# Layer 2 of a four-layer graph kernel: statistics over four batches, small copies on ScalarE, own entries of the mask behind the last sums

## The chip, the cores and the metric

One core of a Trainium2 chip runs the whole program. The metric is the device time of one execution, in microseconds (us). Before the change the median of three runs is 1942.64 us (1941.84 to 1944.92).

Five engines work side by side, each through its own list of instructions in order: TensorE (PE; its weight loads are PEld) multiplies and transposes into the accumulators (PSUM), VectorE (DVE) and ScalarE (ACT) do the elementwise work, GpSimd (POOL) reduces over partitions, SyncE (SP) issues the transfers. They wait for each other by semaphores.

## The reference, cut to what matters

`x` holds 16 batches of 1024 nodes with 64 features, `adj` the 1024 x 1024 adjacency of all batches. Four graph layers follow each other, each in the form `x = layernorm(x + layer(x))`. The change lies in the third, layer 2:

```python
h = inp @ W
s1, s2 = h @ a1, h @ a2                       # one score per node
e = leaky_relu(s1[:, None] + s2[None, :], 0.2)
attention = softmax(where(adj > 0, e, NEG))
x = layernorm(inp + elu(attention @ h))       # mean and variance over the 64 features
```

Layer 3 then uses the same adjacency with its diagonal set (every node is its own neighbour):

```python
mask = graph + eye(N) > 0
scores = where(mask, h @ h.T, NEG)            # four heads, and an outer layer
```

## The kernel before

A batch's 1024 nodes lie as 8 chunks (C) of 128 partitions. The weights aren't formed as a row-wise softmax: since exp(leaky(s1 + s2)) is the larger of two products of exponentials, VectorE builds, for one chunk k of neighbours, `e = max(G, q) * aT` in one instruction over 128 x 1024 (`unit`, L1011). G (exponentials of s1) serves two batches, a *pair*, as do p and q (exponentials of s2 beneath the largest s2); aT is the transposed adjacency in bfloat16. TensorE adds up the products of e with `vals` = x * p over the eight chunks (`product`, L1019); one column of vals holds p itself, so the sums of the softmax come out with the products.

`gat_layer` (L911) writes layer 2's order by hand: for each batch t and chunk k there is a slot. In a slot a unit is issued on VectorE, then the product of the unit two slots back on TensorE, then the slot's tasks in the order in which they were put there. `go` (L1219) emits it in a stretch where the scheduler may not move the four compute engines. So every engine's queue follows the order of the slots, and within a slot the order of the calls of `at`: first the loop over the batches' ends (L1180 to L1189), then the loop over the pairs' preparation (L1191 to L1215). The tasks:

- Ends of batch b (list at L1157, places from L1172): `evict` copies the products yT to SBUF (ACT); `project` multiplies with W and brings the nodes back to partitions (PE, tile po); `divide` (L1083) takes the sums out of po, clamps them on DVE into `sums` (kept for a later check) and takes the reciprocal rt (DVE); `quotients` scales po by rt in eight instructions into v and takes exp(v) into m (ACT); `residual` makes elu and adds x (two DVE instructions); `norm` takes `bn_stats` of each chunk (DVE) and, after each odd batch, `moments` (L754) for the pair's 16 columns; `root` takes the inverse root by Ln and Exp (ACT); `shift` refines it (four DVE instructions with the shift); `store` writes the normalized rows into x by eight ACT instructions (`scaled`, L776; recorded at L780). The last four batches store by two DVE instructions (L1152).
- Preparation of a pair (L1193): `prep_x` transposes x (PE) and copies xT (ACT, L934); `prep_s` makes the scores s1, s2 (PE, tile ps); `prep_top` (L945) copies them to SBUF (DVE), takes the maximum of s2 (DVE) and sends it to POOL for the maximum over partitions, gtop; `prep_p` (L955) makes -gtop and 0.8 gtop (DVE, `down` and `up`) and the exponentials p and q (ACT); `prep_G` (L989) makes s1 for all partitions in two halves (PE, tile pg) and their exponentials G (ACT, L987); `prep_v` (L993) scales x by p into vals in eight ACT instructions and copies p.

Layer 1's last stores (`last`, L2004) and layer 3's first preparation (`ahead`, L2065) are put into layer 2's first and last slots by `extra` (L2093). Layer 3's preparation there is `prep_x` (L1347: transposes, and copies xT at L1354), `prep_h` (L1362: hT), `prep_sq` (L1378: squares) and `shift_of` (L1325). Before layer 3 the diagonal of aT is set in eight DVE instructions (L2105 to L2107), which stand outside the hand-written stretch: the scheduler placed them between layer 2's last units. Layer 3's heads (L1384) then run bursts of scores (PE), exponentials (ACT, L1397), masks (DVE, L1401) and products (PE, L1408).

Of the kernel before, what the change touches and what calls it, by code (L numbers as in the profile page):

```python
# [8 lines left out]
F32 = mybir.dt.float32  # L9
# [4 lines left out]
ALU = mybir.AluOpType  # L14
AX = mybir.AxisListType

P = 128
FLT_MAX = 3.4028234e38
LN_EPS = 1e-5
ALPHA = 0.2  # L20
# [562 lines left out]
def fast_path(  # L583
# [24 lines left out]
    nc = tc.nc  # L608
    B, N, D = x.shape
    C = N // P  # L610
# [3 lines left out]
    GB = 4  # L614
# [6 lines left out]
    small = ctx.enter_context(tc.tile_pool(name="small", bufs=4))  # L621
    ep = ctx.enter_context(tc.tile_pool(name="ep", bufs=2))
# [6 lines left out]
    for g in range(NG):  # L629
        t = xpool.tile([P, C, GB, D], F32, tag=f"x{g}", name=f"x{g}")  # L630
# [16 lines left out]
    ident16 = const.tile([P, P], BF16, tag="ident16", name="ident16")  # L647
# [106 lines left out]
    def moments(st):  # L754


        n = st.shape[1]
        t = {k: small.tile([P, n], F32, tag=f"bn_{k}", name=f"bn_{k}") for k in ("mean", "d", "var", "rstd", "shift")}
        v = nc.vector
        v.tensor_tensor(t["d"], st[:, :, 1], st[:, :, 4], ALU.subtract)  # L760
        v.tensor_tensor(t["var"], st[:, :, 2], st[:, :, 5], ALU.add)
        v.tensor_tensor(t["mean"], st[:, :, 1], st[:, :, 4], ALU.add)

        v.scalar_tensor_tensor(t["d"], t["d"], 0.25, t["d"], ALU.mult, ALU.mult)
        v.tensor_scalar(t["var"], t["var"], 1.0 / D, LN_EPS, ALU.mult, ALU.add)
        v.tensor_tensor(t["var"], t["var"], t["d"], ALU.add)
        root, step = inverse_root(t["rstd"], t["var"])

        def finish():
            step()  # L770
            v.scalar_tensor_tensor(t["shift"], t["mean"], -0.5, t["rstd"], ALU.mult, ALU.mult)  # L771
            return t["rstd"], t["shift"]

        return root, finish
# [136 lines left out]
    def gat_layer(w, name, zero_mean, own, room=None):  # L911
# [33 lines left out]
        def prep_top(b):  # L945
            pt = pq[b]
            s = s12[:, b // 2]
            nc.vector.tensor_copy(s, pt[:, : 4 * C].rearrange("p (c f) -> p c f", f=4))
            top = small.tile([P, 1], F32, tag="top", name="top")
            nc.vector.tensor_reduce(top, s[:, :, 2:4], AX.XY, ALU.max)  # L950
            gtop = small.tile([P, 1], F32, tag="gtop", name="gtop")
            nc.gpsimd.partition_all_reduce(gtop, top, P, bass_isa.ReduceOp.max)
            pq[b] = gtop

        def prep_p(b):  # L955
            gtop = pq[b]
            down = small.tile([P, 1], F32, tag="down", name="down")
            nc.vector.tensor_scalar(down, gtop, -1.0, None, ALU.mult)
            up = small.tile([P, 1], F32, tag="up", name="up")
            nc.vector.tensor_scalar(up, gtop, 1.0 - ALPHA, None, ALU.mult)  # L960
            s2 = s12[:, b // 2, :, 2:4]
            p = small.tile([P, C, 2], F32, tag="p", name="p")
            nc.scalar.activation(p, s2, AF.Exp, bias=down)
            q = small.tile([P, C, 2], F32, tag="q", name="q")
            nc.scalar.activation(q, s2, AF.Exp, bias=up, scale=ALPHA - 1.0)
            pq[b] = (p, q, up)
# [38 lines left out]
        def attention(b):  # L1005
            held = {}
            pair = stats.setdefault(b // 2, {})
            joint = not zero_mean and b < B - 2
            begins, closes = b % 2 == 0 or not joint, b % 2 == 1 or not joint

# [72 lines left out]
            def divide():  # L1083
                pos, tot = held["p"]
                held["v"] = ep.tile([P, C, D], F32, tag="v", name="v")
                if not zero_mean:
                    if begins:
                        n = 2 if joint else 1
                        total = sums[:, b : b + n, :]
                        nc.vector.tensor_scalar(  # L1090
                            total.rearrange("p u (h j) -> p u h j", h=2),
                            pair["tot"].rearrange("p j (u h) -> p u h j", h=2), 1e-30, None, ALU.max,
                        )
                        pair["r"] = small.tile([P, n, C], F32, tag="rt0", name="rt")
                        nc.vector.reciprocal(pair["r"], total)
                    held["r"] = pair["r"][:, b % 2 if joint else 0, :]
                    quotients()
                    return
                total = sums[:, b, :]
                nc.vector.tensor_scalar(total.rearrange("p (h t c) -> p t c h", h=2, t=2), tot, 1e-30, None, ALU.max)  # L1100
                rt = small.tile([P, C], F32, tag="rt", name="rt")
                nc.vector.reciprocal(rt, total)
                held["r"] = rt

            def quotients():
                pos, rt = held["p"][0], held["r"]
                for h, po in enumerate(pos):
                    if zero_mean:

                        for j in range(CH):  # L1110
                            c = h * CH + j
                            nc.scalar.activation(
                                held["v"][:, c, :], po[:, j // 2, j % 2, :], AF.Copy, scale=rt[:, c : c + 1]
                            )
                        continue
                    nc.vector.tensor_tensor(
                        held["v"][:, h * CH : (h + 1) * CH, :].rearrange("p (t c) d -> p t c d", t=2), po,
                        rt[:, h * CH : (h + 1) * CH].rearrange("p (t c) -> p t c", t=2).unsqueeze(3).to_broadcast(
                            [P, 2, 2, D]
                        ), ALU.mult,  # L1120
                    )
                held["m"] = ep.tile([P, C, D], F32, tag="m", name="m", bufs=4)
                nc.scalar.activation(held["m"], held["v"], AF.Exp)

            def residual():
# [3 lines left out]
                nc.vector.scalar_tensor_tensor(m, m, 1.0, v, ALU.min, ALU.add)  # L1129

            def norm():
                if b % 2 == 0:
                    pair["st"] = small.tile([P, 2 * C, 6], F32, tag="bn", name="bn")
                st = pair["st"]
                for c in range(C):
                    nc.vector.bn_stats(st[:, b % 2 * C + c, :], held["m"][:, c, :])
                if b % 2:
                    pair["end"] = moments(st)

            def root():  # L1140
                if b % 2:
                    stats[b // 2]["end"][0]()

            def shift():
                if b % 2:
                    stats[b // 2]["n"] = stats[b // 2]["end"][1]()

            def store():
                rows = slice(b % 2 * C, (b % 2 + 1) * C)
                rstd, shift = (t[:, rows] for t in stats[b // 2]["n"])  # L1150
                if zero_mean and b >= B - 4:
                    nc.vector.tensor_tensor(held["m"], held["m"], bc_last(rstd, D), ALU.mult)  # L1152
                    nc.vector.tensor_tensor(xb(b), held["m"], bc_last(shift, D), ALU.add)
                    return
                scaled(xb(b), held["m"], (rstd, shift), range(C))
# [24 lines left out]
        for b in range(B):  # L1180
            places = ends[b % 2]
            if not zero_mean and b % 2 == 0 and b < B - 2:
                places = [(1, 3), (2, 5), (2, 7), (3, 0), (3, 1), (3, 1), (3, 1), (4, 0)]
            if zero_mean and b == B - 4:
                places = [*places[:-1], (4, 3)]
            if zero_mean and b == B - 1:
                places = [(1, 0), (1, 1), (1, 1), (1, 1), *places[4:]]
            for task, (t, k) in zip(work[b][2], places):
                at(b + t, k, task)  # L1189
# [680 lines left out]
    with tc.tile_pool(name="ps_g", bufs=1, space=bass.MemoryType.PSUM, reuse_waits="tile") as ps_g, tc.tile_pool(  # L1870
# [45 lines left out]
        extra = {}  # L1916
# [173 lines left out]
    with tc.tile_pool(name="ps_g", bufs=1, space=bass.MemoryType.PSUM, reuse_waits="tile") as ps_g, tc.tile_pool(  # L2090
        name="ps_p", bufs=1, space=bass.MemoryType.PSUM, reuse_waits="tile"
    ) as ps_p:
        places = [(15, j) for j in (0, 1, 2, 3, 4, 5, 6, 7)]  # L2093
        extra = {p: [task] for p, task in zip(places, ahead)}
        for p, task in zip(((0, 0), (0, 1), (0, 3), (0, 7), (1, 3), (1, 7)), last):
            extra.setdefault(p, []).append(task)

        ending = l2_go(extra)
    gat.close()
    for j, task in enumerate(ending):  # L2100
        at(0, j, task)

    for c in range(C):  # L2105
        own = aT[:, c, c * P : (c + 1) * P]
        nc.vector.tensor_tensor(own, own, ident16, ALU.max)  # L2107

    early.close()
    l3 = ctx.enter_context(tc.tile_pool(name="l3", bufs=2, reuse_waits="tile"))  # L2110
# [11 lines left out]
    for b in range(B):  # L2122
        units = work[b][0][0] + work[b][1][0]
        outer = outs[b - 1][1][0] if b else []
        for j in range(BURSTS):
            n = (2, 2, 3, 5)[j - 4] if b >= E - 1 and j >= 4 else 5 if j < 4 else 3
            burst, units = units[:n], units[n:]
            m = 5 - n
# [101 lines left out]
```

## Time and profile before

One execution was profiled. Its rows are read against its own time.

| what | us |
|---|---|
| median of three runs | 1942.64 |
| time of the profiled execution | 1941.5 |
| its span, first to last instruction | 1939.5 |
| PE, DVE, ACT, POOL busy in the span | 1869.1, 1762.0, 1322.1, 78.4 |
| DVE units of layers 0 and 2 (L1013, 256) | 315.6, 1275 ns each |
| ACT exponentials of layer 3's heads (L1397, 512) | 538.9, 1123 ns each |
| DVE masks of layer 3's heads (L1401, 512) | 596.1, 1215 ns each |
| ACT rows of `scaled` (L780, 224) | 77.5, 430 ns each |

The first unit of layer 2 starts at 422.7 us, its last at 629.5 us. A timeline row gives start, length, engine, source line, operation, output tile, input tiles, shapes and count; in brackets it may give the idle time before it and what ended that. Tile names leave the layer out (G_l, y_l). A row with a count holds several instructions in a chain: neighbouring instructions of one engine overlap by some tens of ns, so that the distance from start to start, not the length, is what one of them costs its engine.

### The profile page before, as it was taken

What the parts mean: (1) busy time and instruction counts of PE and PEld (TensorE: products, weight loads), DVE (VectorE), ACT (ScalarE), POOL (GpSimd) and SP (SyncE); (2) the same over time, 40 slices, a digit from 0 to 9 for tenths busy, and PEclk for the clock granted to TensorE, in tenths of its full rate; (3) what the DMA queues carried; (4) which work ended last, traced back from release to release, by engine and by line L of the source; (5) the groups of instructions that cost most, each with busy time, mean ns of one, the idle gap of its engine ahead of it and who ended that gap; (6) DMA issues with size and microseconds to landing.
All of it is one profiled execution on the core that took longest, in us unless ns stands there. A gap on an engine that the chain in (4) does not pass through costs nothing. (4 is left out here: it accounts for less than half of the span.)

```text
span 1939.5 us, 25733 instructions
## 1 busy us (share of the span) xinstructions
PE 1869.1 (96%) x9505; PEld 761.3 (39%) x9505; DVE 1762.0 (91%) x2997; ACT 1322.1 (68%) x2316; POOL 78.4 (4%) x77
## 2 busy tenths in 40 slices
PE   8999989989888999999999999999999999999996
PEld 4444347763333333333333333333333333333332
DVE  6899988879999888799998998989989899899997
ACT  4566568767767676777767767677666776776763
POOL 0000000000000000000000000000000000000001
PEclk8999989999999999999999999999999999999998
DMA  7000000000000110000000100000000100001000
GB/s 181 1 1 1 1 1 1 1 1 1 1 1 12 41 59 12 12 16 24 12 18 12 29 17 12 17 18 23 18 12 18 28 12 17 12 18 29 12 23 13
DMA packets 45746, 35.87 MB, mean 18 GB/s; under 512 B 37295, under 2 KB 37616, under 8 KB 45614
## 3 DMA queue, kind: packets, MB, share of 16 engines
q1 hardware_dynamic: 43534, 33.64, 6.6%
q8 instruction: 76, 1.25, 0.3%
q10 hardware_dynamic: 2080, 0.52, 0.1%
q14 instruction: 56, 0.46, 0.1%
HBM read 29.45 MB, written 4.70 MB: 18 GB/s over the span
## 5 line engine op out<-in xcount | busy, mean ns | idle before, releaser
L1397 ACT ACTIVATE e<-s,shift 128x1024 f32<-128x1024 f32 x512 | 538.9, 1123 | 239.2 <-PE s L1393 237.3
L1401 DVE TENSOR_TENSOR e<-e,aT 128x1024 f32<-128x1024 f32 x512 | 596.1, 1215 | 5.9 <-ACT e L1397 5.9
L1393 PE MATMUL s<-hT 64*128 64x512 f32 x2048 | 489.3, 602 | 2.7 <-ACT zT L1440 1.4
L1408 PE MATMUL y<-e,vals 128*64 128x512 f32 x2048 | 483.4, 599 | 2.0 <-DVE e L1401 1.1
L1013 DVE SCALAR_TENSOR_TENSOR e<-G_l,q,aT 128x1024 f32<-128x1024 f32 x256 | 315.6, 1275 | 2.2 <-ACT G_l L987 2.0
L1393 PEld LDWEIGHTS s<-hT 64*128 64x128 f32 x2048 | 183.6, 185 | 288.2 <-issue 143.5
L1025 PE MATMUL y_l<-e,vals_l 128*64 128x512 f32 x1024 | 254.9, 615 | 29.2 <-DVE e L1013 22.4
L1408 PEld LDWEIGHTS y<-e,vals 128*64 128x64 f32 x2048 | 135.2, 136 | 269.1 <-issue 197.8
L1577 DVE TENSOR_TENSOR e<-e,aT 128x1024 f32<-128x1024 f32 x128 | 156.3, 1225 | 11.2 <-ACT e L1564 1.6
L1569 DVE SCALAR_TENSOR_TENSOR junk<-e,aN 128x1024 bf16<-128x1024 f32 x120 | 146.1, 1217 | 0.0
L1564 ACT ACTIVATE e<-s,shift 128x1024 f32<-128x1024 f32 x128 | 138.6, 1114 | 2.4 <-PE s L1559 2.4
L1559 PE MATMUL s<-h2T 64*128 64x512 f32 x512 | 125.8, 591 | 0.0
L1585 PE MATMUL y<-e,h2v 128*64 128x512 f32 x512 | 125.6, 592 | 0.0
L1025 PEld LDWEIGHTS y_l<-e,vals_l 128*64 128x64 f32 x1024 | 61.5, 137 | 161.0 <-issue 76.4
L1950 PE MATMUL po<-hi,aR 128*128 128x512 f32 x256 | 102.6, 402 | 10.1 <-ACT hi L1862 6.3
L1336 POOL PARTITION_ALL_REDUCE gtop<-top x48 | 55.0, 1145 | 1255.9 <-DVE top L1334 985.9
L1950 PE MATMUL po<-lo,aR 128*128 128x512 f32 x256 | 101.0, 395 | 0.0
L780 ACT ACTIVATE x<-m,bn_shift,bn_rstd 128x64 f32<-128x64 f32 x224 | 77.5, 430 | 15.6 <-DVE bn_shift L771 15.6
L1559 PEld LDWEIGHTS s<-h2T 64*128 64x128 f32 x512 | 50.1, 186 | 60.1 <-issue 37.4
L1440 ACT COPY zT<-poT 64x512 f32<-64x512 f32 x124 | 72.0, 581 | 1.1
L1415 ACT COPY yT<-y 128x512 f32<-128x512 f32 x64 | 38.5, 601 | 43.7 <-PE y L1408 42.5
L1585 PEld LDWEIGHTS y<-e,h2v 128*64 128x64 f32 x512 | 36.6, 137 | 73.6 <-issue 58.5
(279 smaller groups left out, 1888.7 us busy)
## 6 DMA issues: line engine op xcount, KB each, us to landing
r<-inverse SPq DMA_DIRECT2D x62, 256.0 KB
adj<-in_adj_dram SPq DMA_DIRECT2D x16, 512.0 KB
out_dram<-res SPq DMA_DIRECT2D x15, 256.0 KB
x<-in_x_dram SPq DMA_DIRECT2D x14, 256.0 KB
rows<-yT SPq DMA_DIRECT2D x62, 4.0 KB
x<-in_x_dram ACTq DMA_DIRECT2D x2, 256.0 KB
sums<-rows SPq DMA_DIRECT2D x31, 8.0 KB
inverse<-rt SPq DMA_DIRECT2D x31, 8.0 KB
```

Of the source, the lines that this page charges most:

```text
L1013: nc.vector.scalar_tensor_tensor(e, G[b - b % 2][:, b % 2, :], pq[b - b % 2][1][:, k, b % 2 : b % 2 + 1], aT[:, k, :], ALU.max, ALU.mult,)
L1025: nc.tensor.matmul(held["y"][h * D : (h + 1) * D, :], vals[b][:, k, :], e[:, h * HALF : (h + 1) * HALF], start=(k == 0), stop=(k == C - 1),)
L1393: nc.tensor.matmul(s[:, i, :], hT[rows, k * P : (k + 1) * P], hT[rows, cols], start=True, stop=True)
L1397: nc.scalar.activation(e, s, AF.Exp, bias=shifts[b, n])
L1401: nc.vector.tensor_tensor(e, e, bc_mid(aT[:, k, h * HALF : (h + 1) * HALF], 2), ALU.mult)
L1408: nc.tensor.matmul(held[h][i * D : (i + 1) * D, :], vals[b][:, k, :], e[:, i, :], start=(k == 0), stop=(k == C - 1),)
L1559: nc.tensor.matmul(s[:, i, :], hT[rows, (i + k // CH) % 2, k % CH * P : (k % CH + 1) * P], hT[rows, 0, :], start=True, stop=True,)
L1564: nc.scalar.activation(e, s, AF.Exp, bias=shifts[b])
L1569: nc.vector.scalar_tensor_tensor(junk.rearrange("p c q -> p (c q)").bitcast(BF16), e.rearrange("p i q -> p (i q)"), 1.0, aN[:, k, :], ALU. ...
L1577: nc.vector.tensor_tensor(e, e, aT[:, k, :].rearrange("p (i q) -> p i q", i=2), ALU.mult)
L1585: nc.tensor.matmul(held["o"][h * D : (h + 1) * D, :], vals["out", b][:, k, :], e[:, h, :], start=(k == 0), stop=(k == C - 1),)
L1950: nc.tensor.matmul(po.rearrange("p q k f -> p (q k f)"), aR[:, k, ic * P : (ic + 1) * P], e[:, k].rearrange("p q k f -> p (q k f)"), start ...
```

## The change

In layer 2 (`zero_mean`) alone, but for the last point:

1. `norm`, `root`, `shift` and `store` work on groups of four batches instead of two, for the first twelve batches; the last four stay in pairs. The statistics' tile of a group has 32 columns, and it and the tile m of those batches come from the layer's own pool, m with 6 buffers. The four stores of a group stand at new places: for its first to last batch at (b + 5, slot 6), (b + 5, slot 0), (b + 4, slot 4), (b + 4, slot 0).
2. `prep_top` takes the maximum straight from PSUM on DVE; the copy of the scores to SBUF goes to ACT, behind it.
3. `prep_p` makes down and up on ACT.
4. `divide` takes the reciprocal straight from PSUM on DVE, without the clamp; the copy of the sums, which only the later check reads, goes to ACT, behind it.
5. The own entries of the mask are set in slot (16, 1), inside the hand-written stretch, behind the last batch's `divide`.

```diff
         def prep_top(b):
...
+            if zero_mean:
+                nc.vector.tensor_reduce(top, got[:, :, 2:4], AX.XY, ALU.max)
+                nc.scalar.copy(s, got)
...
         def prep_p(b):
...
+            if zero_mean:
+                nc.scalar.mul(down, gtop, -1.0)
+                nc.scalar.mul(up, gtop, 1.0 - ALPHA)
...
         def attention(b):
...
+            four = zero_mean and b < B - 4
+            size = GB if four else 2
+            mine = b % size
+            group = stats.setdefault((size, b // size), {})
...
             def divide():
...
-                total = sums[:, b, :]
-                nc.vector.tensor_scalar(total.rearrange("p (h t c) -> p t c h", h=2, t=2), tot, 1e-30, None, ALU.max)
                 rt = small.tile([P, C], F32, tag="rt", name="rt")
-                nc.vector.reciprocal(rt, total)
+                for where, put in ((rt, nc.vector.reciprocal), (sums[:, b, :], nc.scalar.copy)):
+                    put(where.rearrange("p (h t c) -> p t c h", h=2, t=2), tot)
...
-                held["m"] = ep.tile([P, C, D], F32, tag="m", name="m", bufs=4)
+                pool, bufs = (gp, 6) if four else (ep, 4)
+                held["m"] = pool.tile([P, C, D], F32, tag="m", name="m", bufs=bufs)
...
             def norm():
-                if b % 2 == 0:
-                    pair["st"] = small.tile([P, 2 * C, 6], F32, tag="bn", name="bn")
-                st = pair["st"]
+                if mine == 0:
+                    group["st"] = (gp if four else small).tile([P, size * C, 6], F32, tag="bn", name="bn")
+                st = group["st"]
                 for c in range(C):
-                    nc.vector.bn_stats(st[:, b % 2 * C + c, :], held["m"][:, c, :])
-                if b % 2:
-                    pair["end"] = moments(st)
+                    nc.vector.bn_stats(st[:, mine * C + c, :], held["m"][:, c, :])
+                if mine == size - 1:
+                    group["end"] = moments(st)
...
+            if zero_mean and b < B - 4:
+                places = [*places[:-1], ((5, 6), (5, 0), (4, 4), (4, 0))[b % GB]]
...
+        def own_nodes():
+            for c in range(C):
+                own = aT[:, c, c * P : (c + 1) * P]
+                nc.vector.tensor_tensor(own, own, ident16, ALU.max)
+
+        extra.setdefault((B, 1), []).append(own_nodes)
         ending = l2_go(extra)
...
-    for c in range(C):
-        own = aT[:, c, c * P : (c + 1) * P]
-        nc.vector.tensor_tensor(own, own, ident16, ALU.max)
```

`root`, `shift` and `store` use `group` and `mine` in the same way as `norm`.

## The prediction

> **What bounds the kernel now.** I read the stretches by time first, then the waits of VectorE inside layer 2, then the timelines of VectorE and ScalarE over one pair of batches. Columns of the first view: stretch, length, busy time and count of PE, PEld, DVE, ACT, POOL, then clock, DMA share, GB/s.
>
> ```profile
> 430.00:632.00 202.00, 179.83 (x861) 66.50 (x860) 197.53 (x410) 144.25 (x468) 10.54 (x9) 0.99 0.01 3
> 700.00:1300.00 600.00, 599.16 (x2928) 219.33 (x2930) 545.25 (x708) 426.08 (x550) 26.70 (x23) 1.00 0.07 17
> ```
>
> The reader is to see that layer 2 (422 to 634 us) belongs to VectorE, 197.5 of 202 us, and layer 3 to TensorE without a gap. Layer 3 starts from layer 2's last product, so what layer 2 gains or loses moves the end one for one. Next, what VectorE waits for from 422 to 632 us:
>
> ```profile
> DVE e L1013 <- ACT G_l L987: 2.0, 1, 2.0
> ```
>
> One wait in the whole stage: a unit (the product e of one chunk) that waits for ScalarE's exponential G. Apart from that VectorE runs back to back, so its costs are read from start to start of neighbouring rows. VectorE over one pair:
>
> ```profile
> 484.10 0.18 DVE L948 COPY l_s<-ps 128x32 f32<-128x32 f32 x1
> 484.32 0.17 DVE L950 TENSOR_REDUCE top<-l_s 128x1 f32<-128x16 f32 x1
> 484.41 1.28 DVE L1013 SCALAR_TENSOR_TENSOR e<-G_l,q,aT 128x1024 f32<-128x1024 f32 x1
> ...
> 490.15 0.15 DVE L958 TENSOR_SCALAR down<-gtop 128x1 f32<-128x1 f32 x1
> 490.21 0.14 DVE L960 TENSOR_SCALAR up<-gtop 128x1 f32<-128x1 f32 x1
> 490.27 3.67 DVE L1013 SCALAR_TENSOR_TENSOR e<-G_l,q,aT 128x1024 f32<-128x1024 f32 x3
> 493.86 0.16 DVE L1100 TENSOR_SCALAR l_sums<-po 128x8 f32<-128x8 f32 x1
> 494.06 0.20 DVE L1102 RECIPROCAL rt<-l_sums 128x8 f32<-128x8 f32 x1
> 494.18 1.23 DVE L1013 SCALAR_TENSOR_TENSOR e<-G_l,q,aT 128x1024 f32<-128x1024 f32 x1
> 495.33 0.17 DVE L712 SCALAR_TENSOR_TENSOR ln_step<-bn_rstd 128x16 f32<-128x16 f32 x1
> ...
> 496.04 3.67 DVE L1013 SCALAR_TENSOR_TENSOR e<-G_l,q,aT 128x1024 f32<-128x1024 f32 x3
> ```
>
> The third unit of the last row (two starts of 1.19 on: 498.43) is the first of the next pair; it reads the new G. ScalarE beside it:
>
> ```profile
> 493.79 1.11 ACT L987 ACTIVATE G_l<-pg,up 128x1024 f32<-128x1024 f32 x1 [0.60 <-PE pg L978]
> 494.80 1.74 ACT L1112 ACTIVATE v<-po,rt 128x64 f32<-128x64 f32 x8
> 496.57 0.63 ACT L1123 ACTIVATE m<-v 128x512 f32<-128x512 f32 x1
> 497.11 1.10 ACT L987 ACTIVATE G_l<-pg,up 128x1024 f32<-128x1024 f32 x1
> 498.11 2.75 ACT L780 ACTIVATE x<-m,bn_shift,bn_rstd 128x64 f32<-128x64 f32 x8
> ```
>
> The second half of G ends at 498.21, 0.22 us before the unit that needs it. That margin decides this change. The chain to it starts at unit U (490.27): its product and the scores pg on TensorE let G's first half start at U+3.52, and G, eight v, m and G end at U+7.94. VectorE needs it at U+8.16. All seven pairs show it but the first, where ScalarE is late by the 2.0 us above.
>
> **What VectorE saves.**
> - Sums: the clamp goes, the reciprocal reads PSUM itself. Not in the trace; nearest rows: from PSUM 0.16 (clamp), reciprocal 0.20. Start to start 0.32 becomes 0.12 to 0.20; I take 0.12, since the drop of the clamp's hand-over (493.86 to 494.06) is sure: 0.20 a batch.
> - down and up: 490.15 to 490.27, 0.12 to 0.13 a pair.
> - Scores: copy and maximum take 0.31 from 484.10; a maximum straight from PSUM lies between 0.09 (its spacing now) and 0.20; I take 0.10, its own row's: 0.20 saved a pair.
> - Statistics: a pair's cost 0.88 (moments) + 0.71 (495.33 to 496.04) = 1.59. With 32 columns layer 1's tail shows both: 421.69 to 422.72 = 1.03, and 425.11 to 425.89 = 0.78; 1.81 in all. Six pairs become three groups: 6 x 1.59 - 3 x 1.81 = 4.1 us.
> - Own entries: of eight (0.13 each where nothing hides them), six stood ahead of the last unit and cost about 0.3 there. Behind the last reciprocal they take 8 x 0.13 = 1.0 us, in VectorE's idle 3.5 us before layer 3's first mask (637.77): free. Without that cover, 1.0.
>
> Summed over the stage, nearly 10 us. But three new things stand in ScalarE's queue.
>
> **Wait 1: the copy of the sums.** In the changed program's order it stands on ScalarE right ahead of G's first half (even batches) or of the next batch's vals (odd), and it waits for VectorE; v behind it carries no wait of its own any more, so the copy's wait is the one for the reciprocal, issued before it. That ends at U+3.59+0.20; every v in the trace starts 0.10 after rt (453.92+0.20 to 454.22). The copy isn't in the trace: between 0.09 (L999's spacing, 128x8) and 0.47 (L934's, 128x512 from PSUM); nearest is L999, 0.10. So G starts at U+3.99 instead of U+3.52: **0.47 us later**, and v, m and second G behind it.
>
> [...]
>
> In odd batches vals (2.0) now stand behind rt, where they ran before it: from the pair's first unit X, rt at X+8.32, copy, vals, v (1.78), m end at X+13.2, and the residual wants them at X+13.68-0.40 = X+13.28. Just free; I take 0, at worst 0.15 in each of 7 pairs.
>
> **Wait 2: the store ahead of G.** The stores of the first batch of a group are placed in the same slot as the second half of G, and stand first in the order: eight of L780, 498.11 to 500.76 = 2.65 us, ahead of what the next unit needs. It happens three times (G of batches 6, 10, 14).
>
> So, with a hand-over of 0.03 (G's end 445.37 to unit 445.40), the next pair's first unit waits:
> - pairs with a group's end: G at U+8.41+2.65 = U+11.06; VectorE there at 8.16-0.20+0.07 = U+8.03. Stall 3.06.
> - pairs without: G at U+8.41; VectorE at 8.16-0.20-0.71 = U+7.25. Stall 1.19: what the missing step saves is waited away.
>
> Balance of a pair (26.51 now, 471.92 to 498.43). Without group's end: -0.40-0.20-0.13-1.59+1.19 = -1.13. With: -0.40-0.20-0.13+0.15+0.07+3.06 = +2.55. Together +1.42, three times: **+4.3 us**. The other three stores follow within the pair; by the same adding up they delay the copies yT to X+15.9 at most, and the product po needs it at X+17.0: free.
>
> **First pair.** ScalarE is the bound from 435.25 to 445.37. p waits 0.20 for down now; down and up there cost 0.2 to 0.5 (128x1 rows of L1341 last 0.29; p to q is 0.21 apart), and the sums 0.10: **+0.3 us**, and VectorE's savings before it are lost.
>
> **Wait 3: the end.** From the last pair's first unit (X = 604.48) ScalarE runs a store, yT, a store, then the copy after rt (X+8.63), vals, v, m to X+13.07, and now one more store, 2.65, to X+15.7, before the copies xT of layer 3's first transposes. TensorE's phT started at X+14.18 (618.66); it now waits to X+16.3, and all products of batch 15 stand behind it in TensorE's queue. TensorE is busy from there to the last product but for 0.59+0.20 us, so 2.1-0.8 = +1.3 remains; clamp and hand-over less, copy more, -0.1: **+1.2 us**. The queues of SP and POOL keep their order, no transfer moves.
>
> **Sum:** 4.3+0.3+1.2 = +5.8 us. The profiled execution took 1941.5 (span 1939.5 and 2.0 around it): 1947.3. The median of the runs is 1.1 above that execution: **1948.4 us**.
>
> **Rivals.**
> - Faster. Place: the first unit of a pair. If G's second half were there by U+7.25 and U+8.03, nothing would be given back: per four batches -2.32-0.51, three times -8.5, first pair -0.5, end -0.8: -9.8, 1932.8 us. For it: ScalarE idles 3.73 us before p in every pair. Against: that idle lies ahead of pg, which hangs on unit U, and the store's place is fixed. Chance 0.10.
> - No change: the copy holds up nothing (it waits for TensorE only). Stalls 0.73 and 2.60, +1.5 for the three, +0.3, and an end of -0.7, as vals run early: +1.1, 1943.7 us. Against: v lost its wait. Chance 0.17.
> - Slower still: TensorE pauses about 2 and 1.5 us around each long stall. After 5 us of pause (419 to 424) the clock was 0.50 and four products took 5.35 instead of 4.3 us. If each stall brings that, 3 x 1.1, and the residual waits 1.0: +10, 1952.5 us. Chance 0.15. [...]
>
> My forecast has 0.58. The unknown prices (0.2 a pair, 1 at the end) spread it by some 2.5 us. The range, 1943 to 1954, takes in the second and the fourth case. A measurement here tells 0.2%, 3.9 us: faster 0.10; same 0.25 (second rival and the forecast's low edge); slower 0.65.
>
> **What would show it.** VectorE's waits in layer 2: e on G six times beside the first, three near 3.1 and three near 1.2 us; the sums' copy starting 0.1 after each reciprocal, G's first half right behind it; moments three times with 32 columns and two with 16; xT of layer 3 behind a store; pairs of 25.4 and 29.1 us in turn. I am wrong if G's second half ends before its unit, if the copy overlaps the reciprocal, or if VectorE's rows from PSUM cost 0.2 us more than taken.

## The result and the profile after

The changed kernel takes **1951.05 us** (median of nine runs, 1947.68 to 1953.12), beside 1942.65 us (nine runs) for the kernel before: 8.4 us more, a ratio of 1.0040 with a 95% interval of 1.0030 to 1.0051. The forecast was 1948.4.

The profiled execution took 1952.89 us (span 1950.9), 11.4 more than that of before. 8.3 us of it lie in layer 2. Another 1.1 lie ahead of it and 2.0 behind it, where the change alters nothing on the path: over the thirteen profiled kernels of this study, of which all have the same layers 0 and 1, layer 2 starts anywhere from 421.9 to 426.6 us, and the rest behind its last reciprocal takes 1305.2 to 1307.5 us. So layer 2 alone is compared from here on.

The stretches of the changed kernel, with the columns of the prediction's first view:

```profile
430.00:632.00 202.00, 177.59 (x814) 68.77 (x812) 183.64 (x321) 141.96 (x485) 11.05 (x7) 0.94 0.00 1
700.00:1300.00 600.00, 599.16 (x2922) 218.91 (x2922) 545.49 (x709) 426.56 (x549) 26.67 (x23) 1.00 0.06 17
```

In layer 2 VectorE is busy for 183.6 us where it was busy for 197.5, and TensorE's clock has fallen from 0.99 to 0.94; layer 3 is as it was. What VectorE waits for now, from 422 to 645 us:

```profile
DVE e L1026 <- ACT G_l L996: 15.1, 7, 3.4
DVE top L951 <- PE ps L940: 2.1, 2, 1.6
DVE rt L1114 <- PE po L1070: 2.0, 2, 1.1
DVE top L1349 <- PE pn L1345: 0.9, 1, 0.9
```

The one wait for G has become seven: 3.37 us in the first pair, then 1.01, 2.89, 1.02, 2.88, 1.02, 2.88. The other three lines are waits for TensorE, which the forecast didn't have; the kernel before waits 0.4 us for po in this stretch, and for neither ps nor pn. VectorE over the pair that the prediction showed:

```profile
484.50 0.17 DVE L951 TENSOR_REDUCE top<-ps 128x1 f32<-128x16 f32 x1
484.58 1.28 DVE L1026 SCALAR_TENSOR_TENSOR e<-G_l,q,aT 128x1024 f32<-128x1024 f32 x1
...
489.44 0.22 DVE L760 TENSOR_TENSOR bn_d<-bn 128x32 f32<-128x32 f32 x1
...
490.47 3.67 DVE L1026 SCALAR_TENSOR_TENSOR e<-G_l,q,aT 128x1024 f32<-128x1024 f32 x3
494.05 0.20 DVE L1114 RECIPROCAL rt<-po 128x8 f32<-128x8 f32 x1
494.17 1.23 DVE L1026 SCALAR_TENSOR_TENSOR e<-G_l,q,aT 128x1024 f32<-128x1024 f32 x1
495.32 0.18 DVE L712 SCALAR_TENSOR_TENSOR ln_step<-bn_rstd 128x32 f32<-128x32 f32 x1
...
496.10 2.47 DVE L1026 SCALAR_TENSOR_TENSOR e<-G_l,q,aT 128x1024 f32<-128x1024 f32 x2
501.46 1.28 DVE L1026 SCALAR_TENSOR_TENSOR e<-G_l,q,aT 128x1024 f32<-128x1024 f32 x1 [2.89 <-ACT G_l L996]
```

Start to start, the maximum costs 0.08 us, the reciprocal 0.12, the moments with 32 columns 1.03 (489.44 to 490.47) and the step behind them 0.78. The last unit of this pair is done at 498.57; then VectorE stands for 2.89 us. ScalarE in the same stretch:

```profile
494.29 0.17 ACT L1114 COPY l_sums<-po 128x8 f32<-128x8 f32 x1 [3.44 <-DVE rt L1114]
494.35 1.12 ACT L996 ACTIVATE G_l<-pg,up 128x1024 f32<-128x1024 f32 x1
495.36 1.75 ACT L1124 ACTIVATE v<-po,rt 128x64 f32<-128x64 f32 x8
497.15 0.63 ACT L1136 ACTIVATE m<-v 128x512 f32<-128x512 f32 x1
497.68 2.75 ACT L780 ACTIVATE x<-m,bn_shift,bn_rstd 128x64 f32<-128x64 f32 x8
500.34 1.09 ACT L996 ACTIVATE G_l<-pg,up 128x1024 f32<-128x1024 f32 x1
```

ScalarE idles for 3.44 us ahead of the copy, which waits for the reciprocal. Most of this it would idle anyhow, since G's first half needs the scores pg from TensorE; e2_copy_late, where the copy stands further back, has this row in the same place:

```profile
492.72 1.12 ACT L996 ACTIVATE G_l<-pg,up 128x1024 f32<-128x1024 f32 x1 [3.14 <-PE pg L987]
```

The copy's own part is 0.3 us. Then the store stands ahead of G's second half, which ends at 501.43; the unit follows 0.03 later. TensorE's clock around this stall, in windows of 3.41 us (length, then busy time of PE, PEld, DVE, ACT, POOL, then the clock):

```profile
500.05:503.46 3.41, 1.52 (x10) 0.62 (x8) 1.96 (x3) 3.41 (x10) 0.00 (x0) 1.00 0.00 0
503.46:506.88 3.42, 2.26 (x6) 0.29 (x4) 3.42 (x11) 3.42 (x10) 0.00 (x0) 0.50 0.00 0
506.88:510.29 3.41, 3.41 (x14) 2.21 (x14) 3.41 (x5) 1.56 (x6) 0.00 (x0) 0.50 0.02 5
510.29:513.70 3.41, 3.41 (x21) 1.48 (x17) 3.24 (x3) 3.41 (x17) 0.00 (x0) 1.00 0.00 0
```

After the window in which TensorE was busy for 1.52 us, it runs two windows at half clock, falls behind, and the scores for the next pair come 1.60 us late (top at 515.13).

### The profile page after: what moved, and what is told of

The parts are those of the page before. It is cut to its first block, busy times and chain, and to the rows that moved or that the text cites. A ratio compares the mean times of both kernels' runs of the same rounds, so it can differ in the third digit from the quotient of the medians.

```text
span 1950.9 us, 25703 instructions
## 1 busy us (share of the span) xinstructions
PE 1877.3 (96%) x9505; PEld 768.7 (39%) x9505; DVE 1755.2 (90%) x2924; ACT 1324.7 (68%) x2350; POOL 80.6 (4%) x77
## 5 line engine op out<-in xcount | busy, mean ns | idle before, releaser
L1408 PEld LDWEIGHTS s<-hT 64*128 64x128 f32 x2048 | 183.6, 185 | 288.0 <-issue 142.7
```

The costliest lines, as they stand in the source:

```text
L1408: nc.tensor.matmul(s[:, i, :], hT[rows, k * P : (k + 1) * P], hT[rows, cols], start=True, stop=True)
```

## The experiments

Each kernel is the changed one with the edit shown, unless said otherwise. Lengths are from the one profiled execution: *first pair* from layer 2's first unit to the first unit of the second pair, *six pairs* on to the first unit of the last pair, *end* on to the last reciprocal. "Against before" is the difference of the medians, with the kernel before run in turn on the same chip, and the ratio.

| kernel | first pair | six pairs | end | layer 2 | against before, us | ratio (95% interval) |
|---|---|---|---|---|---|---|
| before | 22.68 | 159.08 | 29.55 | 211.3 | | |
| changed | 23.52 | 164.55 | 31.53 | 219.6 | +8.4 | 1.0040 (1.0030 to 1.0051) |
| e1_store_behind_g | 24.17 | 157.14 | 31.51 | 212.8 | +1.3 | 0.9998 (0.9989 to 1.0007) |
| e2_copy_late | 23.52 | 162.57 | 28.88 | 215.0 | +2.5 | 1.0010 (1.0001 to 1.0019) |
| e4_pairs | 23.52 | 156.89 | 28.89 | 209.3 | -3.6 | 0.9980 (0.9971 to 0.9989) |
| e5_stats_only | 23.70 | 163.89 | 29.54 | 217.1 | +4.4 | 1.0019 (1.0010 to 1.0028) |
| e6_pe_busy | 23.51 | 162.25 | 29.86 | 215.6 | +7.5 | 1.0039 (1.0026 to 1.0052) |
| e7_end_store | 23.51 | 164.48 | 28.87 | 216.9 | +5.1 | 1.0023 (1.0013 to 1.0033) |
| e9_g_early | 24.81 | 150.38 | 31.46 | 206.7 | -4.9 | 0.9970 (0.9959 to 0.9980) |
| e8_all | 24.80 | 150.32 | 28.86 | 204.0 | -6.1 | 0.9965 (0.9952 to 0.9978) |
| e10_scores_copy | 22.86 | 164.21 | 29.86 | 216.9 | +5.5 | 1.0035 (1.0022 to 1.0047) |
| e12_first_pair | 22.15 | 150.40 | 28.87 | 201.4 | -10.1 | 0.9948 (0.9936 to 0.9960) |
| e13_pairs_g_early | 21.90 | 154.62 | 28.87 | 205.4 | -6.5 | 0.9966 (0.9954 to 0.9978) |

The lengths hold the falls of TensorE's clock in that one execution. In the first pair the clock is at half for one window of 3.41 us in before, changed, e2, e4, e6, e7 and e10, and for two in the others. The second window costs some 0.65 us, an estimate from two executions: e1_store_behind_g, whose edit doesn't touch the first pair, takes 24.17 there, the changed kernel 23.52.

### e1_store_behind_g

```diff
-places = [*places[:-1], ((5, 6), (5, 0), (4, 4), (4, 0))[b % GB]]
+places = [*places[:-1], ((5, 7), (5, 0), (4, 4), (4, 0))[b % GB]]
```

> One place of the changed kernel altered: the stores of a group's first batch one slot later, (5, 7) for (5, 6), so behind the second half of G in ScalarE's queue; the rest stays. Theory (the store ahead of G is the main loss): G's second half comes 2.65 us earlier in the three pairs with a group's end, VectorE's stall there falls from 2.88 to some 0.3 us, and with it the fall of TensorE's clock that follows these stalls. 3 x 2.6 = 7.8 us, and 2.1 for the two waits of top for the scores at half clock: about 1941 us, a tie with the kernel before or up to 3 us faster. Rival (it is the copy of the sums alone, or VectorE's reads from PSUM, and the store's order moves only who waits): within 2 us of 1951.

The stalls with a group's end fall from 2.88 to 0.23 us, as the theory had it, and the six pairs by 7.4 us. The clock's part was missed: 1941 us was expected, and 1944.24 came, a tie with the kernel before. ScalarE of this kernel, then TensorE:

```profile
501.11 1.10 ACT L996 ACTIVATE G_l<-pg,up 128x1024 f32<-128x1024 f32 x1
502.10 5.40 ACT L780 ACTIVATE x<-m,bn_shift,bn_rstd 128x64 f32<-128x64 f32 x16
507.41 0.57 ACT L934 COPY xT_l<-pxT 128x512 f32<-128x512 f32 x1
507.87 0.58 ACT L1057 COPY yT_l<-y_l 128x512 f32<-128x512 f32 x1
```

```profile
508.51 1.65 PE L1070 MATMUL po<-l_wo,yT_l 128*128 128x130 f32 x8 [1.33 <-ACT yT_l L1057]
```

Two stores in a row now stand ahead of yT, TensorE waits 1.33 us for it, the clock falls to 0.50 from 509.02, and top waits 2.30 us. The store was handed on to the next one in the queue.

### e2_copy_late

```diff
-for where, put in ((rt, nc.vector.reciprocal), (sums[:, b, :], nc.scalar.copy)):
-    put(where.rearrange(...), tot)
+nc.vector.reciprocal(rt.rearrange(...), tot)
...
 nc.scalar.activation(held["m"], held["v"], AF.Exp)
+nc.scalar.copy(sums[:, b, :].rearrange(...), tot)
```

> The changed kernel with the copy of the sums behind m's exponential, at the end of the quotients' task, so that G's first half no longer waits for VectorE's reciprocal; v waits for the reciprocal itself. Theory (the copy's wait delays G): G's first half starts some 0.36 us earlier, at unit + 3.52, the seven waits of e for G are shorter by 0.3 to 0.4 each, and the vals of odd batches run ahead of the reciprocal again: 2.5 us in the pairs and up to 1 at the end, 1947.5 to 1949. Rival (a copy that waits where ScalarE would have waited anyway for the next product costs nothing): within 1 us of 1951.

Five of the six waits for G shrink to 0.70 and 2.57, by 0.31 each, as expected. The other, the second pair's, stays at 1.05: there G's first half waits 1.65 us for pg, just behind a window at half clock. The first pair doesn't move (23.52). The end falls by 2.65 us: 1 us as expected, since the vals of odd batches run while the reciprocal is awaited, and 1.67, because the fall of TensorE's clock at the end doesn't come (see e7_end_store). In the medians the difference against before shrinks by 5.9 us.

### e4_pairs

```diff
-four = zero_mean and b < B - 4
+four = False
...
-if zero_mean and b < B - 4:
-    places = [*places[:-1], ((5, 6), (5, 0), (4, 4), (4, 0))[b % GB]]
```

> The changed kernel with statistics, stores and their places per pair as before; the copies on ScalarE, the reads from PSUM and the own entries stay. Theory: without the store ahead of G the long stalls go, and what VectorE saves on sums, scores, down and up (0.73 a pair) is given back where G is late: G at unit + 8.41 less, VectorE at about unit + 7.5, a wait near 0.9 in each pair, so the pairs get 26.6 to 26.7 us, as long as before. About 1943 to 1945, 6 to 8 us under the changed kernel. Rival (the reads from PSUM and the copies are the loss, not the groups of four): 1948 or more.

Points 2 to 5 alone are 3.6 us **faster** than before: more than expected, because the wait for G is 0.29 in each pair and not 0.9, and the end gains 0.66. The prediction's own terms come near that: VectorE at U+8.16-0.20 = U+7.96, G at U+8.41 less the 0.11 us by which the copy was priced too dear, so U+8.30, a wait of some 0.34.

### e5_stats_only

```diff
-nc.vector.tensor_reduce(top, got[:, :, 2:4], AX.XY, ALU.max)
-nc.scalar.copy(s, got)
+nc.vector.tensor_copy(s, got)
+nc.vector.tensor_reduce(top, s[:, :, 2:4], AX.XY, ALU.max)
...
-nc.scalar.mul(down, gtop, -1.0)
+nc.vector.tensor_scalar(down, gtop, -1.0, None, ALU.mult)
```

In the same way `up`, the sums and the own entries are as in the kernel before.

> The kernel before with point 1 of the change alone, the statistics and stores per group of four: scores, sums, down and up and the own entries as before. Theory: G's halves are not delayed by a copy, but VectorE comes 0.71 earlier in pairs without a group's end (a wait near 0.5) and the store stands ahead of G in the others (a wait near 2.4, with the fall of TensorE's clock behind it). 3 x (2.4 + 0.5) = 8.7 of waits and some 2 of clock against 4.1 saved, and one more store at the end, about 1: 1948 to 1951. Rival (points 2 to 5 carry the loss): 1940 or less.

Point 1 alone (the kernel before with that point) is 4.4 us slower: the waits for G are 0.44 and 2.30 us, and the end stays at 29.54 in spite of its further store. The first pair, 23.70 with no copy in it, goes with a clock at half for two windows there instead of one (l_s waits 0.60 us for the scores). So point 1 carries the loss in the pairs. Points 2 to 4 make each wait for G 0.58 longer: 0.31 is the sums' copy by e2_copy_late; the other 0.27 is taken to be time that VectorE saves and waits away, which no run shows by itself.

The two halves don't add up: points 2 to 5 alone gain 3.6 us, point 1 alone loses 4.4, together they lose 8.4. In the pairs, what VectorE saves by points 2 to 4 is worth something only while G is in time, and point 1 makes it late; at the end the copy of one half meets the store of the other, as e7_end_store shows.

### e6_pe_busy

```diff
+for j in range(CH * 3 if zero_mean and h and b in (8, 12) else 0):
+    nc.tensor.transpose(pt[:, j % CH, :], x_pair(b, h * CH + j % CH), ident)
```

> The changed kernel with the second half of the transposes of x made three more times (results thrown away) for the pairs of batches 8 and 12 alone, so that TensorE works through some 1.8 us of the pause of 1.89 us ahead of the first product after the long stall; nothing else moves. Theory (it is TensorE's idle time around the stall that halves its clock, and the clock that makes VectorE wait for the scores): no fall of the clock behind these two stalls, the waits of top for the scores, 1.60 and 0.49 us in the profiled run, are gone, the pairs behind the stalls get 25.2 us instead of 26.83 and 25.73; about 2 us in all, 1949. The stalls for G stay at 2.9. Rival (the clock's fall has another cause, or costs nothing): pairs and time as they are, or slower by the extra transposes.

TensorE's windows with the first long stall and behind it, cut as before:

```profile
498.61:502.02 3.41, 2.83 (x22) 1.93 (x20) 1.74 (x2) 3.41 (x9) 0.00 (x0) 1.00 0.00 0
502.02:505.43 3.41, 1.97 (x10) 0.48 (x7) 3.38 (x12) 3.41 (x10) 0.00 (x0) 1.00 0.02 5
505.43:508.84 3.41, 3.26 (x19) 1.37 (x18) 3.41 (x5) 1.57 (x6) 0.00 (x0) 1.00 0.00 0
```

With the pause filled the clock stays up behind both stalls, top doesn't wait, and the pairs behind them take 25.14 us as forecast by the theory, instead of 26.83 and 25.73. This is hardly the grid's luck: by the trace, 1.31 us of the first of these windows are busy with the extra transposes alone, so that an estimated 1.52 us would be left without them, as in the changed kernel's window ahead of its fall. In the median only 0.9 us of the 2 show, inside the intervals: the clock need not fall behind a given stall in every execution, as the last section shows.

### e7_end_store

```diff
-places = [*places[:-1], ((5, 6), (5, 0), (4, 4), (4, 0))[b % GB]]
+places = [*places[:-1], ((5, 6), (5, 0), (4, 4), (4, 0 if b < 8 else 3))[b % GB]]
```

> The changed kernel with one store moved: that of batch 11 from (4, 0) to (4, 3), behind the copies xT of layer 3's first transposes. Theory (at the end neither the copy of the sums nor the further store costs anything alone, only both together make xT late): xT some 2.65 us earlier, no pause of 1.91 us in TensorE ahead of phT, the end from the last pair's first unit to the last reciprocal 28.9 to 29.5 us instead of 31.53, the same as with the copy late (28.88) or without the copies (29.54): 2 us, 1949. Rival (the copy alone makes the vals late, and with them all that follows): 31 us, time unchanged.

28.87 us: the end is as short as without the store (28.89, e4_pairs) or with the copy late (28.88, e2_copy_late). The changed kernel's own rows show how the two meet:

```profile
620.48 0.17 ACT L1114 COPY l_sums<-po 128x8 f32<-128x8 f32 x1 [2.81 <-DVE rt L1114]
...
624.84 2.74 ACT L780 ACTIVATE x<-m,bn_shift,bn_rstd 128x64 f32<-128x64 f32 x8
627.49 1.04 ACT L1369 COPY xT<-pxT 128x512 f32<-128x512 f32 x2
```

```profile
628.10 1.60 PE L1382 MATMUL phT<-xT,whT 64*128 64x512 f32 x4 [1.91 <-ACT xT L1369]
629.64 3.60 PE L1038 MATMUL y_l<-e,vals_l 128*64 128x512 f32 x8
```

The copy keeps ScalarE idle for 2.81 us, the store takes 2.65, and xT is late by what neither does alone. The eight products behind phT take 3.60 us, at half clock, where 1.94 is their time at full clock (e10_scores_copy, at 627.63).

### e9_g_early

```diff
-..., (-1, 1), (-1, 4), (-1, 6), (-1, 2), (0, 4)
+..., (-1, 1), (-1, 3), (-1, 5), (-1, 2), (0, 4)
```

> The changed kernel with G's two halves prepared one slot earlier, (-1, 3) and (-1, 5) for (-1, 4) and (-1, 6), so that the second half stands ahead of the store and right behind m; stores, copies and statistics stay as changed. Theory (all that the change loses in the pairs is G being late): the waits of e for G vanish but for the first pair's, pairs of some 24.1 without and 26.0 with a group's end, 3 x (1.02 + 2.88) = 11.7 us less; the first pair and the end keep their 0.8 and 2.0: 1939 to 1941, and 2 more if TensorE's clock stays up. Rival (VectorE is bound elsewhere, so the wait moves to the next thing, as the product's copy yT behind two stores): 1944 or more.

Faster than before, by 4.9 us. From 422 to 632 us VectorE waits for G once, in the first pair:

```profile
DVE e L1026 <- ACT G_l L996: 3.9, 1, 3.9
DVE rt L1114 <- PE po L1070: 1.9, 2, 1.0
DVE top L1349 <- PE pn L1345: 0.9, 1, 0.9
DVE top L951 <- PE ps L940: 0.7, 1, 0.7
```

The six pairs take 150.38 us, 8.7 less than before. The prediction's rival "Faster" had 8.5 for them, on the condition that G is there in time. The change is sound as far as VectorE goes; its time hangs on two places in a list.

### e8_all, e12_first_pair, e13_pairs_g_early

e8_all has the edits of e9_g_early, e2_copy_late and e10_scores_copy (below), and

```diff
-places = [*places[:-1], ((5, 6), (5, 0), (4, 4), (4, 0))[b % GB]]
+places = [*places[:-1], ((5, 6), (5, 2), (4, 4), (4, 0 if b < 8 else 3))[b % GB]]
```

e12_first_pair adds to it

```diff
-for p, task in zip(((0, 0), (0, 1), (0, 3), (0, 7), (1, 3), (1, 7)), last):
+for p, task in zip(((0, 0), (0, 1), (0, 3), (0, 7), (1, 7), (2, 2)), last):
```

e13_pairs_g_early is e12_first_pair with the edit of e4_pairs.

> The changed kernel with every wait found so far moved out of the way: G's halves at (-1, 3) and (-1, 5), the copy of the sums behind m, the copy of the scores with down and up, the second store of a group at (5, 2), that of batch 11 at (4, 3). Theory: no wait for G but the first pair's 2 to 2.5 us, first pair and end as before or shorter by 0.5, the six pairs 24.0 and 25.9 in turn: 9.3 us less than before in the pairs, 0.6 at the end, 1933 us, under both kernels. Rival (what ScalarE has to do in a pair with a group's end no longer fits beside VectorE's 25.9 us, and something else is late): 1937 or more.

> The kernel with all waits moved (e8_all) and two of layer 1's last stores moved from (1, 3) and (1, 7) to (1, 7) and (2, 2), behind the second half of the second pair's G. Theory: the first pair, 24.80 us with a wait of 3.92 for G, loses the store of 2.65 between the vals and G's first half: a wait near 1, about 2.5 us off, 1933.5. Rival (v, which waits for the reciprocal, sets G's second half anyway): a wait above 2.5, under 1.5 us.

> The kernel e12_first_pair with statistics and stores per pair again. Nothing waits for G in either, so the difference is what point 1 of the change is worth by itself. Theory: the steps that VectorE saves, 6 x 1.59 - 3 x 1.81 = 4.1 us, come out whole: 4 us slower than e12_first_pair. Rival (the groups of four cost TensorE pauses or late stores elsewhere): no difference, or under 2 us.

e8_all gives 1935.92 us where 1933 was expected: its pairs and end are as expected, its first pair is not (24.80), since VectorE waits 3.92 us for G and 0.65 for the scores at half clock. In e12_first_pair the wait for G is 1.30 and the first pair 22.15: **1933.59 us, 10.1 under the kernel before**, the fastest of the study. e13_pairs_g_early shows what point 1 is worth when nothing else waits: 154.62 - 150.40 = 4.2 us in the pairs, 3.6 in the medians; the prediction had 4.1.

### e10_scores_copy

```diff
 nc.vector.tensor_reduce(top, got[:, :, 2:4], AX.XY, ALU.max)
-nc.scalar.copy(s, got)
...
+nc.scalar.copy(s, got)
 nc.scalar.mul(down, gtop, -1.0)
```

> The changed kernel with the copy of the scores moved from the maximum's task to that of down and up, so that in the first pair ScalarE no longer waits 2.50 us for the maximum ahead of layer 1's store. Theory (that wait is the first pair's loss): yT of the first batch is copied where TensorE has it ready, 0.76 us earlier, and the first pair, from the first unit of layer 2 to that of the second pair, gets 22.7 to 22.8 us where the clock falls for one window, instead of 23.52; the other pairs stay. 0.8 us, 1950.3; too small for the time, to be read from the trace. Rival (down, up and the sums' copy are the loss): 23.3 us or more.

ScalarE in the first pair of the changed kernel, then of this one:

```profile
434.40 0.19 ACT L952 COPY l_s<-ps 128x32 f32<-128x32 f32 x1 [2.50 <-DVE top L951]
434.48 2.76 ACT L780 ACTIVATE x<-x,bn_shift,bn_rstd 128x64 f32<-128x64 f32 x8
437.14 0.56 ACT L1057 COPY yT_l<-y_l 128x512 f32<-128x512 f32 x1
```

```profile
430.78 2.76 ACT L780 ACTIVATE x<-x,bn_shift,bn_rstd 128x64 f32<-128x64 f32 x8
435.37 0.59 ACT L1058 COPY yT_l<-y_l 128x512 f32<-128x512 f32 x1 [1.83 <-PE y_l L1039]
```

The store no longer waits behind the copy, yT waits for TensorE again, and the first pair takes 22.86 us instead of 23.52. The rest, 0.18 over the kernel before, is what the small work costs ScalarE there: from yT to p 0.81 us instead of 0.69, and 0.05 for the sums' copy. In the median the 0.8 us can't be told.

## Why the prediction was right, and where its terms were off

The direction, the place and the mechanism were right: the store ahead of G's second half and the copy ahead of its first make G late, and VectorE waits away more than it saves. The size came out 2.6 us short, and the terms show two errors of opposite sign: what VectorE and ScalarE do was priced 1.5 us too dear, and TensorE's clock was left out. That the forecast came so near is in part luck: the one error hid some of the other. So is the agreement of the 8.4 us between the medians with the 8.3 in layer 2 of one execution, which is the second slowest of the nine and has 3.1 us more outside layer 2.

In the profiled execution, without the falls of TensorE's clock, the change costs 4.3 us: 0.84 in the first pair, 3 x (25.14 + 28.95) - 159.08 = 3.2 in the six pairs, 29.86 - 29.55 = 0.3 at the end (29.86 is the end in e6_pe_busy and e10_scores_copy, which have the changed kernel's end, and no fall of the clock behind phT). The falls add 1.69 and 0.59 in two pairs and 1.67 at the end, 3.95. Together 8.3.

- **VectorE's savings:** right throughout. Sums 0.20 a batch (0.32 to 0.12), scores 0.23 (0.31 to 0.08) for 0.20, a group's statistics 1.03 + 0.78 = 1.81. Pairs in which nothing waits take 24.13 and 26.0 us in e8_all, e9_g_early and e12_first_pair; the prediction's balance gives 26.51 - 2.32 = 24.19 and 26.51 + 2.55 - 3.06 = 26.00. The own entries stood in VectorE's idle time, as said.
- **Wait 1, the copy of the sums:** right, a little too dear: G's first half starts at U+3.88, not U+3.99, since the copy costs ScalarE 0.06 us and starts 0.03 after the reciprocal's end, where 0.10 was taken for each. (That every v starts 0.10 after rt was misread: it does where ScalarE stands idle for it; at 494.80 in the kernel before G stood in between.) The two overlap in none of the 16 batches of the profiled execution: the copy starts 0.03 us or more behind the reciprocal's end. No run tests why. The "no change" rival, by which it holds up nothing, falls by e2_copy_late: 0.31 us at five of six waits.
- **Wait 2, the store ahead of G:** right: 2.88 and 1.02 measured for 3.06 and 1.19; e1_store_behind_g takes 2.65 of the 2.88 away. The term of +4.3 should have been +3.2: each of the six waits was taken some 0.17 too long, the copy's 0.11 among it.
- **First pair:** mis-sized, 0.84 for 0.3, by a wait that the prediction didn't have. The wait lies in a term that was left out: the prediction priced down, up and the sums' copy, and didn't ask what stands in ScalarE's queue behind the copy of the *scores*, which waits 2.50 us for the maximum with layer 1's store behind it. e10_scores_copy shows it.
- **End:** xT at X+15.57 and phT at X+16.18 for X+15.7 and X+16.3: right. What was taken to remain of it, 1.2 us, is 0.3 at full clock and 2.0 with the fall.
- **The clock:** the forecast has no term for these pauses, so that they cost nothing in it; no run shows that. The rival "slower still" had the fall and 3.3 us for it. The fall came: in the first long stall TensorE paused for 1.89 us, up to 502.81, and from 503.46 its clock was 0.50. It cost 3.95 us in the profiled execution: 1.69 and 0.59 behind the first two stalls, nothing behind the third (at 612.70; the end takes 28.88 us in e2_copy_late with such a fall and 28.89 in e4_pairs without), and 1.67 behind the wait for xT at the end, which that rival didn't have. Its waits of the residual didn't come. Its total, 1952.5, is nearer to the 1951.05 than the forecast's, but for reasons that are in part not its own. e6_pe_busy shows the cause: with TensorE kept busy the clock stays at 1.00 behind these stalls and the waits of top are gone.

## What to carry to other kernels

When small work moves to an engine with time to spare, its cost isn't its length but its place: a copy of 0.06 or 0.08 us that waits for another engine holds up all that stands behind it in the queue (0.31 us at G, 2.5 ahead of a store, 2.8 at the end). Of such a hold-up only that part costs time by which something due comes late: all of the 0.31, some 0.7 of the 2.5, and of the 2.8 nothing until a store stood behind it as well. Time saved on the busiest engine counts only as far as the next thing that it needs comes earlier too; list for each saved stretch who must now be early, and move that first: here two slots for G turned 8.4 us of loss into 4.9 of gain. Moving a long instruction out of the way hands it to the next one in the queue (the store from G to yT), so follow it to a place where nothing due stands behind it.

## What the runs showed of the hardware

In these runs TensorE's clock goes by a fixed grid. In each of the thirteen profiled executions all falls and rises from 3 to 659 us lie on multiples of 3.41 us from one offset; the offset differs from run to run (falls at 503.46, 561.50, 612.70 and 629.76 in the changed kernel are 17, 15 and 5 windows apart; the kernel before has one at 423.80, off that grid). Cut along this grid, from 400 to 656 us, the thirteen profiled executions have 904 windows that begin at full clock. The 32 with the least busy time on TensorE, up to 1.66 us, are each followed by a window at half clock. Of those from 1.68 to 3.40 us none is. So around layer 2 a window with up to 1.66 us busy was enough, and it needn't be one pause: the changed kernel's window from 558.08 us, with 1.47 us busy, holds 0.50 us of one pause and 1.44 of the next.

This border is no rule for the busy time of a profile in general. Ahead of layer 2 the kernel before has windows on the wrong side of it:

```profile
266.79:270.21 3.42, 2.81 (x31) 2.73 (x32) 2.58 (x7) 3.42 (x11) 0.00 (x0) 1.00 0.03 5
270.21:273.62 3.41, 2.19 (x11) 1.78 (x9) 2.24 (x4) 3.41 (x4) 0.00 (x0) 0.50 0.00 0
314.58:317.99 3.41, 1.60 (x12) 1.30 (x11) 3.36 (x7) 2.17 (x4) 0.00 (x0) 1.00 0.00 0
317.99:321.41 3.42, 3.42 (x17) 2.82 (x16) 3.28 (x13) 1.28 (x2) 0.00 (x0) 1.00 0.00 0
```

With 2.81 us busy the clock falls, with 1.60 it stays. From 20 to 1925 us, 17 windows with 1.80 to 2.98 us busy are followed by half clock, one of them in each of the thirteen executions starting between 265 and 271 us; and of the 74 with up to 1.67 us, 18 aren't, all between 313 and 350 us. What the clock counts isn't told by this busy time alone, and stays open.

So the same pauses cost something or nothing by where the grid falls. In e2_copy_late TensorE pauses for 1.57 and 1.45 us behind the first group, and again for 1.57 and 1.44 behind the second:

```profile
498.34:501.75 3.41, 1.84 (x12) 0.62 (x8) 1.87 (x2) 3.41 (x10) 0.00 (x0) 1.00 0.00 0
501.75:505.16 3.41, 1.97 (x11) 0.61 (x8) 3.38 (x12) 3.41 (x11) 0.00 (x0) 1.00 0.00 0
505.16:508.58 3.42, 3.26 (x19) 1.38 (x18) 3.42 (x5) 3.42 (x15) 0.00 (x0) 1.00 0.02 5
```

The first time, above, the grid cuts the idle time in two and the clock stays. The second time, below, 1.24 us of a window are busy, the clock falls, and top waits 1.75 us.

```profile
552.95:556.36 3.41, 1.24 (x6) 0.20 (x4) 2.99 (x4) 3.41 (x11) 0.00 (x0) 1.00 0.00 0
556.36:559.77 3.41, 2.57 (x7) 0.96 (x8) 3.41 (x11) 3.41 (x11) 0.00 (x0) 0.50 0.00 0
```

This fits the spread of the changed kernel's runs, 1947.7 to 1953.1: the four slowest (from 1952.5 us) have a mean granted clock of 0.982 to 0.984, the other five (up to 1951.1) 0.985 to 0.987. Whether the grid's offset makes the whole of that spread is not shown.

One thing more stays open. Of the 904 windows, in ten TensorE counts as busy throughout, and the next is at half clock all the same, as from 536.43 us in the kernel before:

```profile
533.02:536.43 3.41, 3.41 (x24) 2.33 (x24) 3.38 (x6) 2.83 (x12) 0.00 (x0) 1.00 0.03 7
536.43:539.84 3.41, 3.41 (x10) 0.98 (x8) 3.34 (x6) 0.00 (x0) 1.24 (x1) 0.50 0.00 0
```

It comes at most twice an execution in this stretch, in the kernel before too, and in the kernel before nothing waited longer for it there; no run tests what causes it.
